# The last 32 rows of a graph layer's output projection, as one stacked float32r product

## The chip, the cores and the metric

The kernel runs on one core of one Trainium2 chip. The metric is the device time of one execution in microseconds (us), the median of the runs. Five engines work in parallel, each through its own queue in order: TensorE (PE, with its weight loads shown apart as PEld), VectorE (DVE), ScalarE (ACT), GpSimd (POOL) and SyncE (SP, which here only starts DMAs).

## The reference

The inputs are 625 nodes of 1024 features and 20,000 edges of two kinds. The part around the change is a relational graph layer and its output projection; a mixture-of-experts layer follows.

```python
def rgcn_conv(x, edge_index, edge_type, W_rel, W_root, bias):
    h_src = x[src]
    out = x @ W_root + bias
    for r in range(NUM_REL):                      # 2
        w = (edge_type == r).astype(x.dtype)
        msg = h_src @ W_rel[r] * w[:, None]
        sums = segment_sum(msg, dst, num_segments=N)
        cnt = segment_sum(w, dst, num_segments=N)
        out = out + sums / maximum(cnt, 1.0)[:, None]
    return out

y = elu(rgcn_conv(norm_x, ...))                   # 625 x 286  (D_FF = 286)
y = y @ wo_weight                                 # 286 x 1024
return hidden_states + y
...
x = x + _L0_gnn_ref(layernorm(x), ...)
x = x + _L0_ffn_ref(layernorm(x), ...)            # 8 experts, top 2, and 2 shared ones
```

All of it is float32. The contraction of the output projection has 286 rows: two full blocks of 128 and 30 more.

## The kernel before

The 625 nodes are five tiles of 125 rows (`TP = 125`, `NT = 5`). The work runs in these stages.

**Counting** (`one_hots`, `count_windows`, `count_out`, lines 823 to 892). The sums over edges are a product with a matrix of edge counts, CT. For 22 groups of edge columns (`GROUPS`) DVE makes two one-hot tiles, `oh_s` (lines 859 and 860) and `oh_k` (line 863), in a pool `oneh` of six buffers, and PE multiplies them (line 885, `cnt`). When a window of destinations is complete, `count_out` moves it: ACT to integers (line 826), DVE takes the digits apart with a bit mask (line 829), ACT copies them to CT (line 832). The loop calls `between(c)` after each of 160 edge columns c, and a table written by hand, filled with `at(c, f, ...)`, says what else is traced there: transposes of the normed rows, `project` (line 903, the products with the graph weights, fifteen of them, one every 18 columns in the middle of the stage), `add_h` (line 796), `aggregate`, and `clear`. The order on each engine is then fixed at build time from dependences and these places; `tc.issue_after(ins)` keeps an instruction behind another on its own engine.

`project` evicts a product in three steps: ACT to `rest` (line 912), ACT to the rounded `P` (line 913, float32r), DVE the remainder `rest - P` (line 914). So the graph sums already use float32r parts: the product `aggregate` (line 925) multiplies CT in float32r with both parts.

`clear` (lines 1011 to 1016, at column 50) sets the tile `zero` with POOL and writes zeros to the buffer `yt` in HBM with two DMAs of 2.5 MB on SP's queue.

**Aggregate and ELU** (lines 919 to 946). Each tile's sums are scaled and added on DVE; `elu` ends with ACT copying the last 30 columns a second time (line 945), so that the third block of `el` holds them twice, 32 columns apart.

**Output projection** (`elu_columns` and `output_proj`, lines 950 to 982). PE transposes `el` in three pieces (line 956), ACT copies them from PSUM to `eT` (lines 957 and 958), and `output_proj` multiplies per tile and half s of 512 columns: two blocks of 128 rows (line 968), then for both halves the last 30 rows (line 972), on two different groups of 32 rows of the array, the weights `wo_r` laid out to match. DVE adds each half to `xh` (line 975) and runs a layer norm (lines 732 to 736); POOL writes the rows out. The transposes of a normed tile (line 808, `p_t`) follow two tiles later. PE has as further work the shared experts' products (line 1159, `p_sh`), and the gate (line 1107) follows the last tile's transposes.

```python
for t, (c0, c1) in enumerate(((0, 3), (6, 11), (9, 14), (13, 18))):
...
at(50, clear)
...
for i, c in enumerate((3, 12, 15, 20, 38, 56, 74, 92, 110, 128, 146)):
    at(c, project, i + 1)
```

**After it** come routing, shared experts, eleven tiles of expert rows (`p_h`, line 1381; `p_yj`, line 1439) and the sum (`p_o`, line 1494, with a bf16 product of biases in line 1496). Their weights stream in on SP's queue, which starts again at 87.51 us, when the tiles of the `front` pool (node features, graph weights, one-hots, `zero`) are done with.

Of the kernel before, what the change touches and what calls it, by code (L numbers as in the profile page):

```python
# [8 lines left out]
F32 = mybir.dt.float32  # L9
F16 = mybir.dt.float16  # L10
BF16 = mybir.dt.bfloat16
F32R = mybir.dt.float32r
# [6 lines left out]
N = 625  # L19
D = 1024  # L20
E = 20000
R = 2
F = 286
# [3 lines left out]
TP = 125  # L27
NT = N // TP
# [14 lines left out]
QC = 32  # L43
# [16 lines left out]
def dense_kernel(  # L60
# [79 lines left out]
    wo_t = gbig.tile([FK, NFK, D], F32, name="wo_t")  # L140
    FL = F - 2 * FK
    nc.scalar.dma_start(wo_t[:, :2, :], wo[: 2 * FK].rearrange("(t p) m -> p t m", p=FK))
    nc.scalar.dma_start(wo_t[:FL, 2, :], wo[2 * FK :])

# [86 lines left out]

    CT = gbig.tile([128, NM, KEYS], F32, name="CT")
    PASSES = [(0, 418), (418, 418), (836, KEYS - 836)]

    def count_pass(i, between):
# [13 lines left out]
        for m in range(NM):  # L249
            if m % 2:  # L250
                nc.vector.tensor_copy(CT[:, m, c0 : c0 + cn], accs[m][:, :cn])
            else:
                nc.scalar.copy(CT[:, m, c0 : c0 + cn], accs[m][:, :cn])

# [22 lines left out]
    def aggregate(d, r):  # L277
        p = ps_mm(f"p_agg_{d}_{r}")
        at = r * N + d * TP
        for m in range(NM):  # L280
            n = rows_of[m]
            nc.tensor.matmul(p[:TP, : F + 1], CT[:n, m, at : at + TP], P[:n, m, r, :],
                             start=(m == 0), stop=(m == NM - 1))
# [21 lines left out]
    def output_proj(d):  # L305
# [6 lines left out]
        for s in range(2):  # L312
            cols = slice(s * 512, (s + 1) * 512)
            p = ps_acc(f"p_y_{d}_{s}")
            for k in range(NFK):
                n = FK if k < NFK - 1 else FL
                nc.tensor.matmul(p[:TP, :], eT[:n, k, :], wo_t[:n, k, cols],
# [136 lines left out]
def sparse_kernel(  # L454
# [24 lines left out]
    nc = tc.nc  # L479

    def pool(stack, name, bufs=1, side="left", **kw):
        return stack.enter_context(tc.tile_pool(name=name, bufs=bufs, side=side,
                                                reuse_waits="tile", **kw))
# [11 lines left out]
    def ps_acc(name):  # L495
        return psum[0].tile([128, 512], F32, tag="acc", name=name, bufs=nacc[0])

    def ps_mm(name):
        return psum[0].tile([128, 512], F32, tag="mm", name=name, bufs=3)
# [5 lines left out]
    gbig = pool(gnn, "gbig")  # L505
    gsum = pool(gnn, "gsum")
    rows = pool(gnn, "rows", NT)
    grow = pool(gnn, "grow", 2)
# [2 lines left out]
    crow = pool(cnts, "crow", 2)  # L511
    front = ExitStack()
    fbig = pool(front, "fbig", side="right")
    oneh = pool(front, "oneh", 6, side="right")


    PARTS = (slice(0, 112), slice(112, TP))
# [46 lines left out]
    ident = const.tile([128, 128], F32, name="ident")  # L564
# [61 lines left out]
    for i in (2, 3):  # L626
# [5 lines left out]
                                               ap=[[0, 3], [D, NS], [1, D]]))  # L632
    nc.gpsimd.dma_start(bd[:, NS:, :], bass.AP(tensor=b2.tensor, offset=b2.offset,
                                               ap=[[0, 3], [D, NE], [1, D]]))
# [18 lines left out]


    wo_t = gbig.tile([128, 2, D], F32, name="wo_t")
    FL = F - 256
    nc.sync.dma_start(wo_t, wo[:256].rearrange("(t p) m -> p t m", p=128))
    wo_r = gbig.tile([2 * QC, 512], F32, name="wo_r")
    for s in range(2):
        nc.sync.dma_start(wo_r[s * QC : s * QC + FL], wo[256:, s * 512 : (s + 1) * 512])  # L660


    nc.vector.tensor_scalar(low[:, 1], low[:, 0], 1.0 / DEG, 0.5 / DEG - 0.5, op0=ALU.mult, op1=ALU.add)
# [65 lines left out]
    def layernorm(row, h, name):  # L729
        st = small.tile([TP, 2, 6], F32, tag="st", name=name + "s")  # L730
        for s in range(2):
            nc.vector.bn_stats(st[:, s, :], row[:, s * 512 : (s + 1) * 512])
        mv = small.tile([TP, 2], F32, tag="mv", name=name + "m")
        nc.vector.bn_aggr(mv, st.rearrange("p a b -> p (a b)"))
        rstd = rsqrt(mv[:, 1:2], LN_EPS, name + "r")
        nc.vector.tensor_scalar(h, row, mv[:, 0:1], rstd, op0=ALU.subtract, op1=ALU.mult)
# [84 lines left out]


    CT = cbig.tile([TP, NT, R * N], F32R, name="CT")
    def count_out(d, n, acc):
        xi = crow.tile([TP, R * WD], I32, tag="xi", name=f"xi_{d}")[:, : R * n]
        nc.scalar.activation(xi, acc[:, : R * n], AF.Copy, scale=256.0)
        five = [TP, NT, R * n]
        ct = crow.tile([TP, NT, R * WD], I32, tag="ct", name=f"ct_{d}")[:, :, : R * n]
        nc.vector.tensor_tensor(ct, xi[:, None, :].to_broadcast(five),
                                mask[:, :, None].to_broadcast(five), op=ALU.bitwise_and)  # L830
        for r in range(R):
            nc.scalar.copy(CT[:, :, r * N + d : r * N + d + n], ct.rearrange("p t (d r) -> p t d r", r=R)[:, :, :, r])

# [83 lines left out]
    def aggregate(d, r):  # L919
# [3 lines left out]
        for m in range(NT):  # L923
            for i in range(2):
                nc.tensor.matmul(p[:TP, : F + 2], CT[:, m, at : at + TP], P[:, m, r, i],  # L925
                                 start=(m == 0 and i == 0), stop=(m == NT - 1 and i == 1))
# [7 lines left out]
    els = {}  # L934

    def elu(d):
        z = agg[:, d, :]
        lo = grow.tile([TP, F], F32, tag="lo", name=f"lo_{d}")
        nc.vector.tensor_scalar(lo, z, 0.0, None, op0=ALU.min)
        nc.scalar.activation(lo, lo, AF.Exp)  # L940
        el = grow.tile([TP, 256 + 2 * QC], F32, tag="el", name=f"el_{d}", bufs=3)
        nc.vector.memset(el[:, 256:], 0.0)
        nc.vector.tensor_scalar(el[:, :F], z, 0.0, None, op0=ALU.max)
        nc.vector.scalar_tensor_tensor(el[:, :F], lo, -1.0, el[:, :F], op0=ALU.add, op1=ALU.add)
        nc.scalar.copy(el[:, 256 + QC : F + QC], el[:, 256:F])
        els[d] = el

    eTs = {}

    def elu_columns(d):  # L950
        p = ps_mm(f"p_elT_{d}")
        pv = p[:, : 3 * TP].rearrange("p (k n) -> p k n", k=3)
        eT = grow.tile([128, 3, TP], F32, tag="eT", name=f"eT_{d}", bufs=NT - 1)
        for k in range(3):
            n = min(128, 256 + 2 * QC - k * 128)
            nc.tensor.transpose(pv[:n, k, :], els[d][:, k * 128 : k * 128 + n], ident[:TP, :TP])
        nc.scalar.copy(eT[:, :2], pv[:, :2])
        nc.scalar.copy(eT[: 2 * QC, 2], pv[: 2 * QC, 2])
        eTs[d] = eT

    h2s = {}

    def output_proj(d):
        eT = eTs[d]
        ps = [ps_acc(f"p_y_{d}_{s}") for s in range(2)]
        for s in range(2):
            for k in range(2):
                nc.tensor.matmul(ps[s][:TP, :], eT[:, k, :], wo_t[:, k, s * 512 : (s + 1) * 512],  # L968
                                 start=(k == 0), stop=False)
        for s in range(2):  # L970
            r = slice(s * QC, s * QC + FL)
            nc.tensor.matmul(ps[s][:TP, :], eT[r, 2, :], wo_r[r], start=False, stop=True)  # L972
        for s in range(2):
            at = slice(s * 512, (s + 1) * 512)
            nc.vector.tensor_add(xh[:TP, d, at], xh[:TP, d, at], ps[s][:TP, :])  # L975
        h2 = rows.tile([TP, D], F32, tag="h", name=f"h2_{d}")
        layernorm(xh[:TP, d, :], h2, f"ln2_{d}")
        h2s[d] = h2
        for g in PARTS:
            at = slice(d * TP + g.start, d * TP + g.stop)  # L980
            nc.gpsimd.dma_start(h2d[at, :], h2[g, :])
            nc.gpsimd.dma_start(x1d[at, :], xh[g, d, :])  # L982
# [18 lines left out]
    def at(c, f, *args):  # L1001
        after[c].append((f, args))
# [3 lines left out]
            at(c0, stats, t + 1)  # L1006
        at(c1, to_columns, t + 1, None, nT, True)

    zero = fbig.tile([128, D // 2], F32, name="zero")

    def clear():
        nc.gpsimd.memset(zero, 0.0)
        for a in range(2):
            to = bass.AP(tensor=yt.tensor, offset=yt.offset + (a * YB + 1) * D,
                         ap=[[NT * D, 128], [D // 2, 2 * NT], [1, D // 2]])
            nc.sync.dma_start(to, zero[:, None, :].to_broadcast([128, 2 * NT, D // 2]))

    at(50, clear)
    at(30, transpose_vec)
    at(10, scales, 2, 4)  # L1020
    at(14, scales, 4, NT)
# [12 lines left out]
    for d in range(NT - 1):  # L1034
        at(EC - 1, aggregate, d, 1)
        at(EC - 1, elu, d)
        if d > 1:
            at(EC - 1, elu_columns, d - 2)
# [393 lines left out]
    for n, j in enumerate(ORDER):  # L1432
        y = gat.tile([128, D], F32, tag="y", name=f"ys_{j}")
        for s in range(2):
            at = slice(s * 512, (s + 1) * 512)
            p = ps_acc(f"p_yj_{j}_{s}")
            for k in range(HK):
                for a, b, e in parts(j):
                    made = nc.tensor.matmul(p[a:b], hjT[:, j, k, a:b],  # L1439
                                     w2m[j, a, k][:, at] if a else w2a[:, bass.ds(e, 1), k, at],  # L1440
                                     start=(k == 0), stop=(k == HK - 1))
# [12 lines left out]
    for d in range(NT):  # L1454
        for a in range(2):
            at = a * YB + 1 + d * TP
# [24 lines left out]
    for d in range(NT):  # L1481
# [4 lines left out]
        for at in ((0, 512), (512, D)) if d < NT - 1 else ((0, 512), (512, 768), (768, D)):  # L1486
            n = at[1] - at[0]
            at = slice(*at)
            p = (ps_mm if banks % 8 > 4 else ps_acc)(f"p_o_{d}_{at.start}")
            banks += 1  # L1490
            with tc.issue_after(made.ins):
                for i in range(NS):
                    for k in range(HK):
                        nc.tensor.matmul(p[:TP, :n], shT[:, i, k, own], sw2[:, i, k, at],  # L1494
                                         start=(i == 0 and k == 0), stop=False)
# [10 lines left out]
def gnn_ffn_kernel(tc, *args):  # L1506
    nc = tc.nc
    with tc.tile_pool(name="flags", bufs=1) as flags:
        flag = flags.tile([1, 1], I32, name="flag")
        sparse_kernel(tc, flag, *args)  # L1510
        off = nc.values_load(flag, min_val=0, max_val=EC * 4 + 1)
        with tc.If(off > 0):
            dense_kernel(tc, *args)
# [31 lines left out]
```

## Time and profile before

| | |
|---|---|
| median of 3 runs | 298.7 us (298.64 to 299.25) |
| the profiled execution | 299.61 us, span 297.3 us |
| granted TensorE clock, mean | 0.995 |
| busy PE / DVE / ACT / POOL | 287.4 / 165.7 / 102.1 / 43.7 us |
| counting, from the first count to the last | 15.3 to 73.1 us |
| output projection, first product to last | 97.8 to 123.4 us |
| line 968 (two blocks of 128 rows) | 40 instructions in 5 tiles |
| line 972 (the last 30 rows) | 20 instructions in 5 tiles |

The span runs from the first to the last instruction; 2.3 us of the execution lie outside it. A float32 product is two PE instructions in the trace. Instructions on PE overlap, so the length of a run of them is read from the chain of waits, not from their own durations. "Idle before" names what ended the wait of an engine.

### The profile page before, as it was taken

What the parts mean: (1) busy time and instruction counts of PE and PEld (TensorE: products, weight loads), DVE (VectorE), ACT (ScalarE), POOL (GpSimd) and SP (SyncE); (2) the same over time, 40 slices, a digit from 0 to 9 for tenths busy, and PEclk for the clock granted to TensorE, in tenths of its full rate; (3) what the DMA queues carried; (4) which work ended last, traced back from release to release, by engine and by line L of the source; (5) the groups of instructions that cost most, each with busy time, mean ns of one, the idle gap of its engine ahead of it and who ended that gap; (6) DMA issues with size and microseconds to landing.
All of it is one profiled execution on the core that took longest, in us unless ns stands there. A gap on an engine that the chain in (4) does not pass through costs nothing.

```text
span 297.3 us, 4545 instructions
## 1 busy us (share of the span) xinstructions
PE 287.4 (97%) x1583; PEld 190.4 (64%) x1583; DVE 165.7 (56%) x458; ACT 102.1 (34%) x236; POOL 43.7 (15%) x97
## 2 busy tenths in 40 slices
PE   7999999999999999999999999999999999999991
PEld 5877777778888434567777887788743334444451
DVE  6799999998328588838980222132133221157920
ACT  2355115318325422435132553746289111000000
POOL 9400000000000034322021221210012222200000
PEclk9999999999999999999999999999999999999997
DMA  7999910000009999979997344420086545399251
GB/s 216 359 322 389 409 53 0 2 1 2 0 13 337 347 363 395 394 255 338 331 409 315 103 130 126 120 93 2 2 291 249 212 199 225 143 361 376 116 158 50
DMA packets 28657, 61.01 MB, mean 205 GB/s; under 512 B 2176, under 2 KB 16007, under 8 KB 28624
## 3 DMA queue, kind: packets, MB, share of 16 engines
q1 hardware_dynamic: 23102, 43.77, 41.7%
q0 software_dynamic: 5232, 16.55, 15.4%
q10 hardware_dynamic: 296, 0.35, 0.5%
q8 instruction: 15, 0.25, 0.4%
q14 instruction: 12, 0.10, 0.1%
HBM read 42.62 MB, written 18.81 MB: 207 GB/s over the span
## 4 chain that ended last, share of the span: by engine, by line
PE 82%; DVE 14%; ACT 1%; issue 1%; ACTq 0%; DVEq 0%
PE p_h L1381 13%; PE p_yj L1439 13%; PE p_o L1494 12%; PE p_sh L1159 11%; PE p_pr L908 10%; PE p_y L968 6%; PE p_agg L925 4%; PE p_x L1362 3%; DVE ohs L860 2%; DVE ohs L859 2%; PE p_t L808 2%; PE p_y L972 2%; PE scrap L988 2%; DVE st L765 2%; DVE xh L796 2%; DVE ohk L863 1%
## 5 line engine op out<-in xcount | busy, mean ns | idle before, releaser
L908 PE MATMUL p_pr<-wg,nT 128*125 128x286 f32 x240 | 62.1, 409 | 0.2
L908 PEld LDWEIGHTS p_pr<-wg,nT 128*125 128x125 f32 x240 | 43.3, 187 | 12.1 <-ACT nT L814 1.1
L1381 PE MATMUL p_h<-w1a,xsT 128*128 (+2 forms) x176 | 40.0, 380 | 0.0
L1439 PE MATMUL p_yj<-w2a,hjT 128*128 (+2 forms) x88 | 38.6, 594 | 0.0
L1494 PE MATMUL p_o<-sw,shT 128*125 128x512 f32 (+1 forms) x88 | 36.1, 553 | 0.0
L1159 PE MATMUL p_sh<-h2T,sw 128*128 128x313 f32 (+1 forms) x128 | 35.2, 428 | 0.0
L1381 PEld LDWEIGHTS p_h<-w1a,xsT 128*128 128x128 f32 (+2 forms) x176 | 28.7, 168 | 7.4 <-issue 0.5
L1159 PEld LDWEIGHTS p_sh<-h2T,sw 128*128 128x128 f32 x128 | 23.7, 189 | 8.6 <-issue 0.2
L1439 PEld LDWEIGHTS p_yj<-w2a,hjT 128*128 128x128 f32 (+2 forms) x88 | 14.4, 168 | 22.4 <-issue 22.4
L1494 PEld LDWEIGHTS p_o<-sw,shT 128*125 128x125 f32 x88 | 16.4, 187 | 16.9 <-issue 16.2
L1443 DVE COPY ys<-p_yj 128x512 f32<-128x512 f32 x15 | 10.4, 692 | 28.7 <-PE p_yj L1439 27.1
L1385 DVE COPY hj<-p_h 128x256 f32<-128x256 f32 x11 | 4.7, 425 | 31.1 <-PE p_h L1381 31.1
L982 POOL DMA_DIRECT2D x1d<-xh x10 | 5.4, 540 | 95.7 <-DVE xh L975 95.7
L1447 POOL DMA_INDIRECT yt<-ys,row x11 | 10.8, 981 | 50.5 <-DVE ys L1443 50.5
L968 PE MATMUL p_y<-wo_t,eT 128*125 128x512 f32 x40 | 18.1, 595 | 0.0
L1354 POOL DMA_INDIRECT xs<-h2d,tok x11 | 10.6, 961 | 45.6 <-PE p_x L1362 30.9
L1396 ACT ACTIVATE hjT<-p_hT,vT 128x128 f32<-128x128 f32 (+2 forms) x34 | 8.7, 332 | 24.5 <-PE p_hT L1393 24.5
L1366 DVE COPY xsT<-p_x 128x512 f32<-128x512 f32 x11 | 7.6, 692 | 17.0 <-PE p_x L1362 14.7
L1470 DVE SCALAR_TENSOR_TENSOR x<-p_o,x 125x512 f32<-125x512 f32 (+1 forms) x11 | 6.9, 641 | 16.3 <-PE p_o L1496 16.3
L925 PE MATMUL p_agg<-P,CT 125*125 125x288 f32 x100 | 15.6, 306 | 0.0
L912 ACT ACTIVATE rest<-p_pr,sc 125x286 f32<-125x286 f32 x10 | 5.0, 500 | 29.5 <-PE p_pr L908 22.0
L1381 PE MATMUL p_h<-w1m,xsT 128*64 128x256 f32 (+1 forms) x96 | 14.7, 381 | 0.0
(306 smaller groups left out, 423.8 us busy)
## 6 DMA issues: line engine op xcount, KB each, us to landing
w1a<-in_L_ffn_W_dram SPq DMA_DIRECT2D x8, 1024.0 KB, 12.1
w2a<-in_L_ffn_W_dram SPq DMA_DIRECT2D x8, 1024.0 KB, 6.5
yt<-zero SPq DMA_DIRECT2D x2, 2560.0 KB
g<-yt SPq DMA_DIRECT2D x10, 512.0 KB, 7.2
sw<-in_L_ffn_sW_dram SPq DMA_DIRECT2D x4, 1024.0 KB, 5.0
x<-x1d SPq DMA_DIRECT2D x5, 500.0 KB
wg<-in_L_gnn_W_rel_dram SPq DMA_DIRECT2D x2, 1144.0 KB, 17.1
x1d<-xh POOLq DMA_DIRECT2D x5, 448.0 KB, 6.4
```

The costliest lines, as they stand in the source:

```text
L908: nc.tensor.matmul(p[:TP, :F], nT[:, k, m * TP : (m + 1) * TP], wg[:, k, r, :], start=(k == 0), stop=(k == KD - 1))
L925: nc.tensor.matmul(p[:TP, : F + 2], CT[:, m, at : at + TP], P[:, m, r, i], start=(m == 0 and i == 0), stop=(m == NT - 1 and i == 1))
L968: nc.tensor.matmul(ps[s][:TP, :], eT[:, k, :], wo_t[:, k, s * 512 : (s + 1) * 512], start=(k == 0), stop=False)
L1159: nc.tensor.matmul(p[:, : z - a], sw1[:, i, k, t * 128 : (t + 1) * 128], h2T[:, k, a:z], start=(k == 0), stop=(k == KD - 1))
L1354: nc.gpsimd.indirect_dma_start(out=xs, out_offset=None, in_=h2d, in_offset=bass.IndirectOffsetOnAxis(ap=tok[:, j : j + 1], axis=0))
L1362: nc.tensor.transpose(p[:, k * 128 : (k + 1) * 128], xs[:, at : at + 128], ident)
L1381: nc.tensor.matmul(p[a:b, :H], xsT[j][:, k, a:b], w1m[j, a][:, 0, k, :] if a else w1a[:, bass.ds(e, 1), k, :], start=(k == 0), stop=(k == ...
L1396: nc.scalar.activation(hjT[:, j, t, a:b], p[:, t * 128 + a : t * 128 + b], AF.Gelu, bias=bT[:, bass.ds(e, 1), t])
L1439: made = nc.tensor.matmul(p[a:b], hjT[:, j, k, a:b], w2m[j, a, k][:, at] if a else w2a[:, bass.ds(e, 1), k, at], start=(k == 0), stop=(k = ...
L1443: nc.vector.tensor_copy(y[:, at], p)
L1447: sent.append(nc.gpsimd.indirect_dma_start(out=yt, out_offset=bass.IndirectOffsetOnAxis(ap=row[:, j : j + 1], axis=0), in_=y, in_offset=No ...
L1494: nc.tensor.matmul(p[:TP, :n], shT[:, i, k, own], sw2[:, i, k, at], start=(i == 0 and k == 0), stop=False)
```

## The change

The last rows become 32 instead of 30: the second block of 128 rows is cut to 126 (rows 128 to 253), and rows 254 to 285 form the third. `el` holds these 32 columns four times, so one transpose puts them on all 128 partitions. The copy `eR` is float32r, and on its upper 64 partitions DVE replaces the rounded value by the remainder. The weights `wo_r` are loaded four times over, rounded by ACT, and POOL replaces the second and the fourth group of 32 rows by the remainder. One float32r product of 128 rows then sums all four combinations of parts. Each half s gets its three products in a row, where before the last rows of both halves came at the end.

The weights' parts are made in `last_rows`, at column 78: for each half a DMA fills `zero` (now also the buffer of the load), ACT rounds it, behind the last copy to CT traced until then, and POOL subtracts twice on 32 partitions. `clear` moves from column 50 to 82. The pool of one-hots goes from six buffers to five. `clear` itself, all stages after the output projection and all other shapes are as before.

```diff
-    oneh = pool(front, "oneh", 6, side="right")
+    oneh = pool(front, "oneh", 5, side="right")
...
-    FL = F - 256
+    FL = F - QC
     nc.sync.dma_start(wo_t, wo[:256].rearrange("(t p) m -> p t m", p=128))
-    wo_r = gbig.tile([2 * QC, 512], F32, name="wo_r")
-    for s in range(2):
-        nc.sync.dma_start(wo_r[s * QC : s * QC + FL], wo[256:, s * 512 : (s + 1) * 512])
+    wo_r = gbig.tile([128, D], F32R, name="wo_r")
+    zero = fbig.tile([128, 512], F32, name="zero")
+
+    def last_rows():
+        for s in range(2):
+            at = slice(s * 512, (s + 1) * 512)
+            nc.sync.dma_start(zero, bass.AP(tensor=wo.tensor, offset=wo.offset + FL * D + s * 512,
+                                            ap=[[0, 4], [D, QC], [1, 512]]))
+            with tc.issue_after(outs[-1].ins):
+                nc.scalar.copy(wo_r[:, at], zero)
+            for g in (1, 3):
+                r = slice(g * QC, (g + 1) * QC)
+                nc.gpsimd.tensor_sub(wo_r[r, at], zero[r], wo_r[r, at])
...
         for r in range(R):
-            nc.scalar.copy(CT[:, :, r * N + d : r * N + d + n], ct.rearrange("p t (d r) -> p t d r", r=R)[:, :, :, r])
+            outs.append(nc.scalar.copy(CT[:, :, r * N + d : r * N + d + n],
+                                       ct.rearrange("p t (d r) -> p t d r", r=R)[:, :, :, r]))
...
-        el = grow.tile([TP, 256 + 2 * QC], F32, tag="el", name=f"el_{d}", bufs=3)
-        nc.vector.memset(el[:, 256:], 0.0)
+        el = grow.tile([TP, FL + 128], F32, tag="el", name=f"el_{d}", bufs=3)
...
-        nc.scalar.copy(el[:, 256 + QC : F + QC], el[:, 256:F])
+        nc.scalar.copy(el[:, F:].rearrange("p (g f) -> p g f", g=3),
+                       el[:, FL:F][:, None, :].to_broadcast([TP, 3, QC]))
...
-        eT = grow.tile([128, 3, TP], F32, tag="eT", name=f"eT_{d}", bufs=NT - 1)
-        for k in range(3):
-            n = min(128, 256 + 2 * QC - k * 128)
-            nc.tensor.transpose(pv[:n, k, :], els[d][:, k * 128 : k * 128 + n], ident[:TP, :TP])
-        nc.scalar.copy(eT[:, :2], pv[:, :2])
-        nc.scalar.copy(eT[: 2 * QC, 2], pv[: 2 * QC, 2])
-        eTs[d] = eT
+        eT = grow.tile([128, 2, TP], F32, tag="eT", name=f"eT_{d}", bufs=NT - 1)
+        eR = grow.tile([128, TP], F32R, tag="eR", name=f"eR_{d}", bufs=NT - 1)
+        for k, a in enumerate((0, 128, FL)):
+            nc.tensor.transpose(pv[:, k, :], els[d][:, a : a + 128], ident[:TP, :TP])
+        nc.scalar.copy(eT, pv[:, :2])
+        nc.scalar.copy(eR, pv[:, 2])
+        nc.vector.tensor_sub(eR[64:], pv[64:, 2], eR[64:])
+        eTs[d] = eT, eR
...
         for s in range(2):
+            at = slice(s * 512, (s + 1) * 512)
             for k in range(2):
-                nc.tensor.matmul(ps[s][:TP, :], eT[:, k, :], wo_t[:, k, s * 512 : (s + 1) * 512],
-                                 start=(k == 0), stop=False)
-        for s in range(2):
-            r = slice(s * QC, s * QC + FL)
-            nc.tensor.matmul(ps[s][:TP, :], eT[r, 2, :], wo_r[r], start=False, stop=True)
+                n = min(128, FL - k * 128)
+                nc.tensor.matmul(ps[s][:TP, :], eT[:n, k, :], wo_t[:n, k, at], start=(k == 0), stop=False)
+            nc.tensor.matmul(ps[s][:TP, :], eR, wo_r[:, at], start=False, stop=True)
...
-    zero = fbig.tile([128, D // 2], F32, name="zero")
...
-    at(50, clear)
+    at(78, last_rows)
+    at(82, clear)
```

## The prediction, made before the changed kernel was run

> **What bounds the kernel now.** I read the page first, then the chain of waits, then the timelines of the two stretches that the change touches. PE is busy for 287.4 of 297.3 us, so a change pays where it takes work from PE, or one of its few waits, and costs where it makes PE wait. The chain of waits through the last tile of the output projection, and three short runs from elsewhere in it:
>
> ```profile
> 77.07 1.33 PE p_agg L925 x10
> ...
> 118.94 3.44 PE p_y L968 x8
> 122.38 1.10 PE p_y L972 x4
> 123.48 0.68 DVE xh L975
> ...
> 127.64 0.82 DVE h L736
> 128.60 1.04 PE p_t L808 x8
> ...
> 258.22 0.22 PE p_o L1496
> ```
>
> A tile costs 3.44 us for its four full products, 0.86 each, and 1.05 to 1.10 us for the last 30 rows of both halves. The chain then leaves PE for DVE's layer norm; PE's own timeline shows what it does meanwhile:
>
> ```profile
> 123.36 1.96 PE L808 MATMUL p_t<-ident,h 125*128 125x125 f32 x16
> 125.16 2.80 PE L1159 MATMUL p_sh<-h2T,sw 128*128 128x313 f32 x10
> 128.60 1.04 PE L808 MATMUL p_t<-ident,h 125*128 125x125 f32 x8 [0.64 <-DVE h L736]
> ```
>
> Of DVE's 5.1 us only 0.64 is idle on PE. Now the middle of the counting stage, where the new weights' parts are made. The table by stretches (PE, PEld, DVE, ACT, POOL, then clock, DMA share and GB/s), PE's one wait there, and three lines of ACT's timeline:
>
> ```profile
> 37.00:58.00 21.00, 21.00 (x161) 16.27 (x159) 20.50 (x38) 7.51 (x20) 0.00 (x0) 1.00 0.06 23
> 58.36 0.36 PE L885 MATMUL cnt<-ohk,ohs 125*128 125x58 f16 x7 [0.20 <-DVE ohk L863]
> 51.47 1.65 ACT L832 CAST CT<-ct 125x315 fp32r<-125x315 int32 x4
> 53.01 0.43 ACT L913 CAST P<-rest 125x286 fp32r<-125x286 f32 x1
> ...
> 60.28 0.50 ACT L912 ACTIVATE rest<-p_pr,sc 125x286 f32<-125x286 f32 x1 [3.97 <-PE p_pr L908]
> ```
>
> DVE is busy for 20.5 of 21 us and its one-hots come just as PE takes them: the group of columns 104 to 111 is ready at 58.31 and PE had waited for it. ACT has room, DMA moves nearly nothing, POOL rests. Last, the only place where POOL reads two tensors while DVE works, from both engines' timelines (the third line is the same DVE form, alone):
>
> ```profile
> 7.38 0.67 DVE L778 TENSOR_SCALAR h<-xh,neg 125x640 f32<-125x640 f32 x1
> 7.42 0.26 POOL L625 TENSOR_TENSOR join<-ident 128x32 f32<-128x32 f32 x1
> 14.80 0.55 DVE L778 TENSOR_SCALAR h<-xh,neg 125x640 f32<-125x640 f32 x1
> ```
>
> **The change part by part.**
>
> *Last rows on PE.* A float32r product of 288 columns takes 0.133 us in a run (1.33 over 10), a bf16 one of 512 takes 0.22 (line 1496, between float32 products). By columns 0.133 gives 0.24; I take 0.225. A tile loses about 1.05 and gains 0.45: 0.60 saved, five times, 3.0 us. Cutting the second block to 126 rows I cost at nothing, since a run's length goes with columns. The weight loads (0.19) lie under the product before, as in line 1496's runs; should they not, it is at most 0.19 a tile. The third transpose loads 128 columns instead of 64: 140 against 110 ns, under 0.15 in all, partly hidden.
>
> *The wait at the end.* Half 0 is now complete 1.9 us (two products of 0.86 and one of 0.225) ahead of half 1, so its addition (0.68) and statistics (0.69) run beside half 1, and the norm ends 3.7 instead of 5.1 us after the last product. PE has 4.5 us to do there, so the 0.64 goes and no more. What is late next is DVE: its tile takes 4.65 us (107.52 to 112.2), PE's new one 3.9 plus 0.5 (transposes of `el`) or 1.0 (`p_t`). Laid out from 97.84, PE reaches the last `p_t` at about 124.9, and DVE's last norm, with two new subtractions of at most 0.35 (line 1110, 128x125 from PSUM), ends at 124.7. Before it was 128.60. Bounds: 0 to 0.64; I take 0.64.
>
> *Ahead of the first product.* ACT's copy of `el` grows from 30 to 96 elements, 0.217 to at most 0.256 us (line 958, 125 elements); `eR` is a copy like line 958's. DVE drops a memset of 0.11 and gains up to 0.35 per tile. Two of these may come in DVE's order before line 944 of the third tile, for which PE waits 0.61 at 96.93. Between 0 and 0.5 lost, I take 0.2. For tiles 3 and 4 `eR` is ready 6 us and more before its use.
>
> *Making the weights' parts.* On ACT: two copies of 128x512, 0.64 each (line 1375). The first comes behind the copies to CT that end at 53.12 and line 913, when ACT has nothing until 55.34: nothing lost. On SP: two loads of 256 KB replace two of 60; the second waits until POOL has read `zero`. Behind it on SP stand `clear`'s two DMAs, issued at 18.57 before and now after the last subtraction and POOL's memset (0.54), near 65. They took 5.7 us to issue and move 5.2 MB, 14 us at the 375 GB/s of the later loads; the queue has nothing else until 87.51, and `yt` is wanted after 217. Were that cover gone, the shared weights (line 1078), issued by 100.9 and landing 5.0 us later, would have 19 us until their first use at 125.16, more than the 14. The early DMAs lose `clear`'s traffic, which stood behind them: no gain counted. Fewer one-hot buffers: in the trace each group's line 859 begins after the group five before it was used; the closest is the one begun at 41.8, whose fifth predecessor is done at about 41.7. So nothing, at most 0.2.
>
> On POOL: four subtractions of 32x512, reading two tensors. The row is line 627, 128x32 in 0.266 us; the Trainium skill, "GPSIMD Engine Reference", section "Performance versus the Vector engine", gives 4497 ns for 2048 elements, which with that row is 2.1 ns an element, 1.27 us each (an estimate). POOL has the time. DVE may not. The row: with POOL's 0.26 beside it, line 778 took 0.67, alone 0.55, so DVE lost 0.12, 45% of POOL's time. The skill, "SBUF — State Buffer", section "Who interferes with whom", speaks against this change: a DVE instruction with two SBUF inputs and a GpSimd instruction that reads SBUF exclude each other for the whole instruction. Lines 859, 860, 863, 796 and 914 all have two. By the rule DVE loses 1.27 per subtraction, by the row 0.57, and 0 if POOL's reads fit in DVE's gaps. The first pair falls at about 54 to 57, where DVE has no slack: what it loses, PE waits. The second falls past 61; the next group (ready 64.05, used 64.60) has 0.55 of slack. So the cost is 2h + max(0, 2h - 0.55): 0 for h = 0, 1.7 for 0.57, 4.5 for 1.27. I take the row: it is one pair, but of this chip.
>
> **Sum.** -3.0 - 0.64 + 0.2 + 1.7 = -1.7 us. Against the profiled execution's 299.61 this is 297.9; that one stood 0.9 above the median, and I subtract from the median: 297.0.
>
> **The rivals.**
>
> *No collision.* POOL's reads cost DVE nothing. For it: DVE's two-input rows were never seen beside POOL's. Then -3.4: 295.3.
>
> *The port held for the whole subtraction*, the slower case. At 54 to 57 and 61 to 64 DVE's one-hots wait 1.27 us for each subtraction, PE behind them: -3.44 + 4.5 = +1.1, 299.8. It decides from h = 1.0, where 4h - 0.55 equals the gain. For it stands the rule; against it the row, whose DVE instruction lost less than half of POOL's time.
>
> *ACT's queue held.* ACT's second copy waits for the second load, behind it the eviction that starts at 60.28, then DVE's line 914 and the one-hots. If DVE keeps POOL out until it stops itself at 61.3, two subtractions (2.5), a load (3.9 us for 512 KB of `xh`), the copy and lines 912 and 913 follow: about 7.5 us of PE waiting, 302.8 or more. The lead of the second copy, which I put near 60, is about nothing, so half a us of this may come in any case.
>
> *The stacked product isn't cheap.* Were float32r two passes of 0.43, a tile would save 0.19 instead of 0.60, and the sum be +0.35: 299.1. Line 925's 0.133 us for 288 columns speaks against it.
>
> **How the numbers follow.** What a measurement here can tell from no change is about 0.2%, 0.6 us: faster is below 298.1, slower above 299.3. Partial collision, h from 0.3 to 0.8, gives 296.0 to 298.0: 0.40, the likeliest. No collision, 294.7 to 296.0: 0.25. Port held, 298.1 to 300.4: 0.20, of which 0.07 lies within 0.2%. ACT held, over 300.4: 0.09. Product not cheap: 0.06, mostly same. That makes faster 0.66, same 0.12, slower 0.22. The range 294.8 to 300.4 leaves out ACT's case and the edges.
>
> **What would show it.** Right: a run of two float32r instructions per tile near 0.22 each in place of line 972, tiles of 4.4 to 4.9 us, PE's wait for line 736 near zero, the last `p_t` 3.4 us nearer to the first `p_y`. For the collision: lines 859 to 863 longer than 0.68 and 0.39 beside POOL's four subtractions, and PE waiting for `ohk` between 55 and 65. Wrong: PE waiting for `ohk` by 4 us or more, or ACT idle before the second copy while line 912 is due; or the four subtractions beside DVE rows of unchanged length, and a time near 295.

## The result, and the profile after

The change made the kernel slower: 302.63 us median (301.52 to 303.84), beside 298.75 us for the kernel before on the same chip, a ratio of 1.0125 [1.0081, 1.0169]. In a second set of runs (e9 below) it was 302.45 against 299.03, ratio 1.012 [1.0071, 1.017]. 297.0 was predicted. The profiled execution took 301.66 us (span 299.9) at a mean clock of 0.988, where before had 0.995.

First the chain of waits of the changed kernel, from the last long run of the aggregate to the first tile of the output projection (start, length, what):

```profile
89.12 6.53 PE p_agg L938 x49
...
96.88 0.30 DVE eR L972
...
97.95 0.30 DVE eR L972
...
99.78 0.45 ACT lo L953
...
100.75 0.27 ACT el L957
101.02 0.07 ACT deg L940
...
101.13 0.20 PE p_deg L719 x2
101.33 3.47 PE p_y L984 x4
104.80 0.36 PE p_y L985
105.16 1.72 PE p_y L984 x4
106.88 0.23 PE p_y L985
```

Before, the same place read:

```profile
97.64 0.20 PE p_deg L709 x2
97.84 3.63 PE p_y L968 x8
101.47 1.05 PE p_y L972 x4
```

Two things stand out in the chain of the changed kernel. The new product (line 985) is cheap: 0.23 us for a half tile at 106.88, where before took 1.05 for both halves of line 972. But the full products of the first half tile take 3.47 us, those of the second 1.72: for that stretch PE ran at half its speed. The mean granted clock from 101.30 to 104.80 us is 0.53; in the 4.3 us before it is 1.00. The row of granted clock on the page of the changed kernel has a dip in the same place (before, all slices but the last were 9):

```profile
PEclk9999999999999799999999999999999999999997
```

Next PE's timeline, the rows in which it waited by 0.8 us or more after the start of the counting stage (idle time and releaser in brackets):

```profile
55.43 0.39 PE L898 MATMUL cnt<-ohk,ohs 125*128 125x58 f16 x8 [2.11 <-DVE ohk L876]
...
66.31 0.20 PE L898 MATMUL cnt<-ohk,ohs 125*128 125x24 f16 x2 [0.84 <-DVE ohk L876]
...
98.94 0.55 PE L969 MATMUL p_elT<-ident,el 125*128 125x125 f32 x3 [0.89 <-DVE el L956]
...
101.13 0.20 PE L719 MATMUL p_deg<-deg,onec 125*1 125x10 f32 x2 [1.64 <-ACT deg L940]
...
129.87 1.04 PE L818 MATMUL p_t<-ident,h 125*128 125x125 f32 x8 [0.93 <-DVE h L746]
```

Before, the longest from there on were 0.64 for `h` and 0.61 for `el`, and `p_deg` waited 0.20:

```profile
96.93 0.51 PE L956 MATMUL p_elT<-ident,el 125*128 125x125 f32 x3 [0.61 <-DVE el L944]
97.64 0.20 PE L709 MATMUL p_deg<-deg,onec 125*1 125x10 f32 x2 [0.20 <-ACT deg L927]
```

The first two waits of the changed kernel are for one-hots that came late. DVE's and POOL's timelines show why: POOL's subtractions (line 670) begin at 52.11 and at 60.53, and four groups of DVE instructions are longer than the same forms elsewhere, two of which are shown for comparison.

```profile
52.11 3.01 POOL L670 TENSOR_TENSOR wo_r<-zero,wo_r 32x512 fp32r<-32x512 f32 x2 [41.12 <-ACT wo_r L667]
60.53 3.54 POOL L670 TENSOR_TENSOR wo_r<-zero,wo_r 32x512 fp32r<-32x512 f32 x2 [5.41 <-ACT wo_r L667]
```

```profile
52.25 1.75 DVE L873 TENSOR_TENSOR ohs<-ohs,cols 125x1024 f16<-125x1024 f16 x1
53.92 1.46 DVE L876 TENSOR_TENSOR ohk<-iota,cols 125x464 f16<-125x464 f16 x1
...
57.47 0.68 DVE L873 TENSOR_TENSOR ohs<-ohs,cols 125x1024 f16<-125x1024 f16 x1
58.07 0.39 DVE L876 TENSOR_TENSOR ohk<-iota,cols 125x464 f16<-125x464 f16 x1
...
61.43 1.51 DVE L927 TENSOR_TENSOR P<-rest,P 125x286 fp32r<-125x286 f32 x1
62.86 2.36 DVE L872 TENSOR_TENSOR ohs<-iota,cols 125x1024 f16<-125x1024 f16 x2
```

1.75 against 0.68, 1.46 against 0.39, and by other rows of the same timeline 1.51 against 0.44 and 2.36 against 1.28: each subtraction cost DVE 1.07 or 1.08 us, whatever the instruction beside it. That is 2.09 ns for each of its 512 elements. While one of the two engines reads, the other waits; this is the shared port of which the prediction speaks.

So the change has two new costs ahead of the stage that it speeds up, and the stage's gain is there. The table puts the stages of the profiles side by side. The counting stage runs from the `p_t` for which PE waits near 28 us to the run of 49 `p_agg`; the start from there to the first `p_y`; the output stage from the first `p_y` to the last `p_t`. Lengths of stages can be compared even where the runs reached them at different times.

| | before | after | difference |
|---|---|---|---|
| counting | 27.99 to 87.44: 59.45 | 25.91 to 89.12: 63.21 | +3.76 |
| start of the output projection | to 97.84: 10.40 | to 101.33: 12.21 | +1.81 |
| output stage | to 128.60: 30.76 | to 129.87: 28.54 | -2.22 |
| `p_sh` done while PE waits for the last norm | 10 instructions | 8 | +0.53 later |
| sum | | | +3.88 |

The medians differ by 3.88 as well. That they agree so closely is luck. The two profiled executions themselves differ by only 2.05 us (301.66 and 299.61), because in the changed one these stages began 2.08 earlier: what lies ahead of these stages ended anywhere from 25.9 to 30.2 us in the profiles of this study, and 5.2 to 7.8 us lay between the start of the last addition and the end of the span, for all kernels. The experiments are therefore read by stage first, and by their medians second.

### The profile page after: what moved, and what is told of

Its sections match the earlier page's. It is cut to its first block, busy times and chain, and to the rows that moved or that the text cites. A ratio compares the mean times of both kernels' runs of the same rounds, so it can differ in the third digit from the quotient of the medians.

```text
span 299.9 us, 4534 instructions
## 1 busy us (share of the span) xinstructions
PE 283.9 (95%) x1573; PEld 190.4 (63%) x1573; DVE 171.3 (57%) x458; ACT 103.4 (34%) x238; POOL 50.2 (17%) x101
## 4 chain that ended last, share of the span: by engine, by line
PE 77%; DVE 18%; ACT 1%; issue 1%; ACTq 0%; DVEq 0%
PE p_h L1393 13%; PE p_yj L1451 13%; PE p_pr L921 13%; PE p_o L1506 11%; PE p_sh L1171 11%; PE p_agg L938 4%; PE p_x L1374 3%; PE p_y L984 2%; DVE ohs L872 2%; DVE ohs L873 2%; DVE xh L988 2%; DVE st L775 2%; PE scrap L1001 1%; DVE ohk L876 1%; DVE h L746 1%; PE p_t L818 1%
## 5 line engine op out<-in xcount | busy, mean ns | idle before, releaser
L984 PE MATMUL p_y<-wo_t,eT 128*125 128x512 f32 (+1 forms) x40 | 20.5, 637 | 0.0
L873 DVE TENSOR_TENSOR ohs<-ohs,cols 125x1024 f16<-125x1024 f16 (+1 forms) x22 | 14.9, 676 | 0.0
L872 DVE TENSOR_TENSOR ohs<-iota,cols 125x1024 f16<-125x1024 f16 (+1 forms) x22 | 14.7, 684 | 0.0
L938 PEld LDWEIGHTS p_agg<-P,CT 125*125 125x125 f32 x100 | 13.9, 187 | 0.8 <-DVE P L927 0.5
```

The source lines that it names most:

```text
L872: nc.vector.tensor_tensor(os, row[:, None].to_broadcast(shape), key, op=ALU.is_equal)
L873: last = nc.vector.tensor_tensor(os, os, both(VV_, 128)[1], op=ALU.mult)
L984: nc.tensor.matmul(ps[s][:TP, :], eT[:n, k, :], wo_t[:n, k, at], start=(k == 0), stop=False)
```

## The experiments

**e1 and e11: the change without POOL's subtractions.** The weights' low parts are left out, as in e3, in e10 and partly in e7, so these kernels show times and are no replacement for the change.

```diff
-            for g in (1, 3):
-                r = slice(g * QC, (g + 1) * QC)
-                nc.gpsimd.tensor_sub(wo_r[r, at], zero[r], wo_r[r, at])
```

> The changed kernel without POOL's four subtractions, so the low parts of the weights are not formed (groups 2 and 4 of wo_r hold the rounded value again). Theory: the subtractions keep DVE's two-input instructions waiting by 1.07 us each (lines 873, 876, 927 and 872 were longer by that beside them), and PE waited 2.11 + 0.28 + 0.84 = 3.2 us for one-hots; all of it goes: 302.6 - 3.2 = 299.4, with PE's wait for check's product (1.64 us) and the slow first product of the output projection still there. Rival, all of the loss lies in the wait ahead of the output projection: 302.6, the gaps in counting filled by something else. Rival, one-hots are late because of five buffers instead of six: gaps of 2 us in counting remain.

300.24 us (ratio to before 1.0031 [1.0009, 1.0053]). The counting stage is back at 59.53 us, and both waits for one-hots are gone. The wait for `deg` (1.65) and the slow half tile (3.48) remain. So POOL's subtractions are all of the counting stage's 3.7 us, and the other two belong to something else. The same kernel on another chip:

> The change without POOL's subtractions (the weights' low parts are left out) once more, on the chip of the other two. Theory: 300.2, 2.4 to 4 us below the change, with the first half tile at 3.47 us again. Rival (that half tile's 3.47 us was an accident of one run): 1.72 us, and 298.5.

300.37 us, 1.0041 [1.0007, 1.0075], with the slow half tile again.

**e2: the change, with `check` traced later.** The product `p_deg` sums the node degrees to see whether the edge list is as expected. In the changed kernel it stands ahead of the first `p_y`, and PE waits 1.64 us for it. The order on ACT has changed: before, its last copy of `deg` came right behind the fourth tile's exponential (`lo`, 97.10 to 97.54) and ahead of that tile's copy of `el`; now it comes behind both. ACT's timeline before:

```profile
97.10 0.44 ACT L940 ACTIVATE lo<-lo 125x286 f32<-125x286 f32 x1
97.45 0.14 ACT L927 COPY deg<-p_agg 125x1 f32<-125x1 f32 x1
98.07 0.22 ACT L945 COPY el<-el 125x30 f32<-125x30 f32 x1 [0.48 <-DVE el L944]
```

In the chain of the changed kernel `lo` ends at 100.23 and `deg` starts at 101.02.

```diff
-            check()
...
+        if s == 0:
+            check()
```

> The changed kernel with check(), whose one small product waits for the last copy to deg on ACT, traced after the first tile's output projection instead of before it. Theory: PE then waits only for the transposes of the third tile, 1.4 us less, and since it no longer stands nearly idle for 3 us the clock isn't lowered and the first half tile takes 1.72 instead of 3.47 us: together about 3.2, 299.4. Rival, the clock falls for another reason: 1.4 us only, 301.2. Rival, the port alone costs the time: 302.6.

303.46 us (1.0159 [1.0103, 1.0215]): no gain, where 299.4 was expected. Inside the trace the edit did its work: from the `p_agg` run to the last `p_t` it takes 38.43 us against 40.75. The clock fell in another place, in the counting stage, right after PE's wait of 2.11 us for one-hots at 56.07. Its row of granted clock:

```profile
PEclk9999999899999999999999999999999999999997
```

That fall cost little: the stage took 63.53 us beside 63.21 in the changed kernel. Its stages add up to +1.9 us over before, and the profiled execution was longer by 1.8 (301.40 beside 299.61); it was the fastest of four. The other three took 302.97 to 304.22 and left no trace, so why the median is 4.1 above before's is not explained, and the gain shows in the stages alone.

**e3: both edits.**

> Both edits: no subtractions on POOL (the weights' low parts are left out) and check() after the first tile's output projection. Theory: the two losses add, 302.6 - 3.2 - 3.2 = 296.2 or a little less, which is before's 298.75 minus the 3 us and more of PE work saved. Rival, one stall hides in the other: about 299.

297.04 us (0.9924 [0.9901, 0.9947]), with no dip in the clock row: counting 59.53, then 38.44 to the last `p_t` against 41.16 before. With both new waits away, the faster product is worth about 2 us.

**e4: the kernel before, with five one-hot buffers.**

> The kernel before with five one-hot buffers instead of six, nothing else. Theory: no group waits for a buffer, 298.75 within 0.5. Rival, DVE's lead is cut: over 299.5, with gaps before line 885 in counting.

298.97 us, 0.9994 [0.997, 1.0019]; counting 59.54. The smaller pool costs nothing, as the prediction had it.

**e7: less reading on POOL, one profile.**

```diff
-                nc.gpsimd.tensor_sub(wo_r[r, at], zero[r], wo_r[r, at])
+                if s == 0:
+                    half = slice(0, 256)
+                    nc.gpsimd.tensor_sub(wo_r[r, half], zero[r, half], wo_r[r, half])
+                else:
+                    nc.gpsimd.memset(zero[r], 0.0)
```

> One look at the port in the change: the first pair of POOL's subtractions is half as wide (32x256), and the second pair is replaced by two POOL memsets of 32x512 that read nothing (so part of the weights' low parts is left out). Theory (POOL holds the port for the elements that it streams, about 2.09 ns each): the DVE instruction beside each half-wide subtraction is 0.53 us longer, so ohs at line 873 takes about 1.2 and ohk at 876 about 0.9, and those beside the memsets are 0.68, 0.39 and 1.28 as without POOL. Rival A (a fixed hold per POOL instruction): 1.07 longer for the half-wide ones too. Rival B (POOL's writes hold DVE as well): 0.5 to 1.1 us longer beside each memset.

POOL's and DVE's timelines:

```profile
54.50 3.98 POOL L672 TENSOR_TENSOR wo_r<-zero,wo_r 32x256 fp32r<-32x256 f32 x2 [42.70 <-ACT wo_r L667]
64.26 1.09 POOL L674 MEMSET zero<- 32x512 f32 x2 [5.78 <-ACT wo_r L667]
```

```profile
56.14 1.75 DVE L810 SCALAR_TENSOR_TENSOR xh<-h,rstd,xh 125x1024 f32<-125x1024 f32 x1
57.82 0.98 DVE L931 TENSOR_TENSOR P<-rest,P 125x286 fp32r<-125x286 f32 x1
...
65.05 0.46 DVE L931 TENSOR_TENSOR P<-rest,P 125x286 fp32r<-125x286 f32 x1 [2.31 <-ACT P L930]
```

The half-wide subtractions held other instructions than expected (lines 810 and 931), but for the expected time: 0.47 (1.75 against 1.28 for line 810 at 52.47) and 0.52 (0.98 against 0.46). Half the elements, half the hold; so there is no fixed hold per instruction (1.8 to 2.1 ns an element). Beside the memsets line 931 takes its plain 0.46: POOL's writes held nothing here. What the hold is, is now settled; *when* POOL gets the port is not. Two half-wide subtractions took 3.98 us here, two whole ones 3.01 in the changed kernel: from POOL's start at 54.50 it was 1.6 us until the first DVE instruction that it held (line 810, 56.14), and DVE worked without a gap meanwhile.

**e6: ten products in the wait for `deg`.**

```diff
+        for _ in range(10):
+            nc.tensor.matmul(p[:, 128:256], ident, ident, start=True, stop=True)
```

> The change with ten extra 128x128 products on PE (their results are used by nothing) ahead of the check's product, in the 1.6 us in which PE waits for deg; nothing else differs. Theory (the first half tile of the output projection takes 3.47 instead of 1.72 us because PE had little to do in the 3 us ahead of it and its clock fell): it takes 1.72 us, the clock's row shows 9s there, and the time falls by up to 1.9 us, to about 300.8. Rival (the clock's fall follows from something else, such as the 2.1 us wait in the counting stage, or the products only lengthen PE's own work): no change or longer, 302.6 to 304.

305.61 us (1.021 [1.0147, 1.0273]), a miss in the total. The first half tile did speed up, to 1.91 us. But the counting stage, which the edit doesn't touch, took 64.66 instead of 63.21. POOL's, ACT's and PE's timelines of e6:

```profile
54.79 5.06 POOL L670 TENSOR_TENSOR wo_r<-zero,wo_r 32x512 fp32r<-32x512 f32 x2 [41.84 <-ACT wo_r L667]
```

```profile
64.78 0.62 ACT L667 CAST wo_r<-zero 128x512 fp32r<-128x512 f32 x1 [7.88 <-DMA zero<-in_L_gnn_wo_weight_dram]
...
65.83 0.43 ACT L928 CAST P<-rest 125x286 fp32r<-125x286 f32 x1
```

```profile
66.41 0.37 PE L940 MATMUL p_agg<-P,CT 125*125 125x288 f32 x1 [1.22 <-ACT P L928]
```

Here POOL got the port late. So it freed `zero` late, the second load came late, and ACT stood 7.88 us in front of its second copy, with the eviction of `project` queued behind; PE waited 1.22 us for that. This is the prediction's rival of ACT's queue, at a sixth of its price. e7 shows it too (1.33 us); the changed kernel's own profile does not.

**e10: the same ten products, without POOL's subtractions.**

> The change without POOL's subtractions (the weights' low parts are left out), and with the ten extra 128x128 products on PE in the wait for deg. Theory (the clock falls because PE has too little to do in those 3 us): first half tile 1.72 to 1.9 instead of 3.47 us; the products themselves end 0.5 later than the wait did, so 1.0 to 1.2 us less than the same kernel without them, about 299.2 beside 300.2. Rival (the clock's fall is a matter of the run): no difference between the two, or 0.5 more.

This is the clean test of the clock, beside e11 on the same chip: 298.08 us (0.996 [0.9929, 0.9991]) against 300.37 (1.0041 [1.0007, 1.0075]); the intervals don't meet. The chains of the two, e11 first:

```profile
99.61 3.48 PE p_y L981 x4
```

```profile
99.02 2.24 PE p_deg L717 x20
...
101.38 1.91 PE p_y L983 x4
```

Giving PE *more* to do made the kernel faster. From the `p_agg` run to the last `p_t` it is 39.57 instead of 40.63 us, the 1.1 expected; the medians differ by 2.3, and the other 1.2 isn't placed. The clock is on record for every run, not only for the two that left a trace: the mean of a run was 0.996 to 1.000 in all twelve of e10 and 0.984 to 0.993 in all twelve of e11. It was 0.994 to 1.000 in all twenty of e3, which has no wait for `deg`, and 0.983 to 0.993 in all twenty of e1, which has it.

**e9: the change once more.**

> The change once more, unaltered, for its spread on one chip beside the next two. Theory: POOL's four subtractions and DVE's instructions contend for the port, and when POOL gets it is a matter of how the two fall in time. Where POOL gets it at once, as in the change's first profile, the counting stage loses 3.8 us; where it gets it 1.6 us later, as in the profile with the products in the wait, the second load and with it ACT's second copy come late and the stage loses about 5.1 us. So the profile shows one of the two, 63.2 or 64.4 to 64.7 us from the first p_t after the wait for h to the p_agg run of 49, and the times spread over 2 us, 301.5 to 304. Rival (the longer stage belongs to the edit of those two runs, not to the change): 63.2 and 301.5 to 302.7.

302.45 us (301.06 to 303.92). The counting stage took 63.24 us, so the longer form didn't appear in this profile either; and the first half tile took 1.91 us:

```profile
103.35 1.91 PE p_y L984 x4
```

The waits ahead of it were the same, 0.88 and 1.65 us. So the clock's fall is not certain: of the five profiles with both of these waits and no extra products (after, e1, e7, e9, e11) four have it there. (The mean clock of this run was 0.993. The other five runs of e9 and the four of the changed kernel had 0.982 to 0.989, so those probably had it too.) Its price can be read from e9 against the first profile: 39.06 against 40.75 us to the last `p_t`, 1.7 us. Whether the 64.7 us of e6 also occur in the unaltered change stays open: both profiles are of short executions. Of its ten runs five took 301.06 to 301.84 us, these two among them, and five took 303.06 to 303.92, without a trace.

**e5: the whole change in another place.**

```diff
-    at(78, last_rows)
-    at(82, clear)
+    at(50, clear)
...
+    at(EC - 1, last_rows)
...
-            check()
...
+        if s == 0:
+            check()
```

> All of the change is kept, in another place: the weights' parts are made behind the last of the copies of counts (slot EC-1, where DVE has no one-hots left to make), clear goes back to slot 50, and the check of the degrees follows the first tile's output projection. Theory (port collision in the counting stage plus the check's product held on PE): the counting stretch is 59.5 us again as in before, POOL's four subtractions touch no one-hot, the first half tile runs at full clock, and the time is that of the run without subtractions and with the late check, about 297.0 (296.5 to 297.6). Rival (the parts cost their time wherever they stand, since something waits for them or for their loads): 299 or more, with PE waiting for wo_r at the first p_y or DVE's z and lo steps 1.07 us longer per subtraction and PE waiting for el.

298.05 us (0.9951 [0.9923, 0.998]), half a per cent below before and clearly below the change as it was, though 1.0 above what was expected. By stage it is e3 to the hundredth: counting 59.53, then 38.44. The 1.0 lies outside these stages and isn't explained. POOL's subtractions now run where DVE has no one-hots to make, and in 1.37 us each (POOL's timeline, the first pair; then DVE's, one line; then PE's, its longest wait):

```profile
78.02 2.73 POOL L670 TENSOR_TENSOR wo_r<-zero,wo_r 32x512 fp32r<-32x512 f32 x2 [66.05 <-ACT wo_r L667]
```

```profile
87.61 0.75 DVE L927 TENSOR_TENSOR P<-rest,P 125x286 fp32r<-125x286 f32 x1 [7.03 <-ACT P L926]
```

```profile
126.91 1.04 PE L818 MATMUL p_t<-ident,h 125*128 125x125 f32 x8 [1.74 <-DVE h L746]
```

The hold is still there: line 927 begins in the middle of a subtraction of the second pair and takes 0.75 instead of 0.46. But DVE has stood idle 7.03 us ahead of it, and PE doesn't wait. The 1.74 shows the next bound: DVE's layer norms.

**e8: e5, with the norm's last step on ACT** (for the last tile half on each engine).

```diff
-        nc.vector.tensor_scalar(h, row, mv[:, 0:1], rstd, op0=ALU.subtract, op1=ALU.mult)
+        if cut:
+            nc.vector.tensor_scalar(h[:, :cut], row[:, :cut], mv[:, 0:1], rstd, op0=ALU.subtract, op1=ALU.mult)
+        nb = small.tile([TP, 1], F32, tag="neg", name=name + "nb")
+        nc.vector.scalar_tensor_tensor(nb, mv[:, 0:1], -1.0, rstd, op0=ALU.mult, op1=ALU.mult)
+        nc.scalar.activation(h[:, cut:], row[:, cut:], AF.Identity, bias=nb, scale=rstd)
```

> The version of the run before the last two (parts made late, check after the first tile) with one more edit: the last step of the second layer norm, h = (x - mean) * rstd over 1024 columns, goes from DVE to ACT (for the last tile half on each). Theory (with the faster product DVE's norms bound the output stage, and PE's wait of 1.75 us for h at line 746 is their surplus): DVE loses 0.8 us per tile, the wait falls to under 0.6 and the time to about 295.7 (1 to 1.5 us below that version). Rival (ACT takes longer for it, 1.0 us or more, and the last tile's norm ends no earlier, or ACT's copies of h2T stand behind it): the same time or up to 1 us more, 297 to 298.

297.44 us (0.9942 [0.991, 0.9974]). In the profile the gate's first product comes 38.16 us after the `p_agg` run, in e5 39.49, so the step is worth 1.3 there: PE's wait for the norm falls from 1.74 to 0.74 us, though ACT takes 1.24 us per tile for what DVE did in 0.81. The medians differ by only 0.6, and the intervals overlap, so a gain over e5 isn't shown.

## Why the prediction was wrong

The sum said -1.7 us, and the stages give +3.9. Three of its steps failed. The hold h on DVE's one-hots was taken as 0.57 us and measured 1.07, which is 2.1 us of the miss. The start of the output stage was taken as 0.2 and measured 1.81, another 1.6, since the wait for `deg` was not seen. The fall of the clock behind that wait was put at nothing and cost 1.7. The small rest of the miss, 0.3, lies in the output stage. A right h alone would have moved the sum to +0.3, 299.0 us, which the prediction itself would have called the same.

**The product: right.** In e9, where the clock stayed up, the output stage took 26.86 us against 30.76, so 3.90 less. Of this 0.53 is `p_sh` work that only moved to a later place; 3.37 remain, and 3.64 were predicted (3.0 of products and 0.64 of the wait). A product took 0.23 where 0.225 was taken. That the transposes beside it also got shorter (`p_elT` 0.32 instead of 0.47) was not in the sum.

**The collision: the mechanism right, its size wrong.** This is the term h. The row chosen was one pair in which DVE lost 0.12 us beside a POOL instruction of 0.26, read as 45% of POOL's time, so 0.57 for one of 1.27. Measured: 1.07. The row could not carry this. Its DVE instruction (line 778) reads one tensor and a column of scalars, where the one-hots read two tensors, and its POOL instruction streams 32 elements, where the new one streams 512. Scaled by elements instead of by time, its 0.12 would have given 1.9, too much. It doesn't even repeat: in e4 line 778 begins at 7.53, beside the same POOL instruction (7.41 to 7.68), and takes its plain 0.55. The sum's own formula, 2h + max(0, 2h - 0.55), gives 3.73 with h = 1.07, and the stage lost 3.76. So the slack was right, and so were the places, and only h was not. The Trainium skill's page "SBUF — State Buffer", section "Who interferes with whom", against which the row was preferred, calls the port an exclusive lock, held for the whole instruction; the hold measured is 1.07 us of the 1.37 that an undisturbed subtraction takes in e5. It was nearer than the row: with its 1.27 the prediction's rival gave 299.8, still without the start and the clock.

**The start: 0.2 predicted, 1.81 measured.** This step looked at what DVE and ACT do for `el`, and found 0.28 of the loss (the wait for `el` grew from 0.61 to 0.89). It did not ask what PE has in line ahead of the first `p_y`. There stands `p_deg`, which had waited only 0.20 for its last `deg`. In the changed kernel the last `deg` comes behind `el` on ACT, which is 0.79 us of delay (100.23 to 101.02). And `lo` itself starts 4.13 us after the end of the aggregate's run where it was 3.14, with DVE's two new subtractions in that chain, 0.30 each (line 972). Together that is 1.78 of the 1.81; the wait for `deg` grew by 1.44. The bound of 0 to 0.5 was drawn around the edited instructions, not around the order that they stand in.

**The clock: not foreseen.** Before the first `p_y` PE was idle 0.89 and 1.64 us in a little over 3 us, and in four profiles of five the next half tile ran at half speed, 1.7 us lost. e10 shows that PE's idleness is the cause: filled with useless products, the wait is followed by products at full speed. So do e2 and e3, where the wait is gone and the first half tile is as short as the later ones. The skill's page "TensorE: Matmul & The Clock Gate", section "What's actually happening", gives a window of about 3.4 us of idling after which the clock halves. The traces agree with the halving (3.47 against 1.72) and with the time scale, but here it fell although PE was not fully idle, and in e9 with the same two waits it did not.

**The tail: half right.** The end of DVE's last norm was laid out at 26.9 us after the first `p_y`; e9 has 26.86 to the last `p_t`. But PE had got there earlier than laid out, with shorter tiles and two `p_sh` instructions fewer to do, and so waits 0.93, where the prediction let the whole 0.64 go. The two instructions come back later as 0.53.

**What cost nothing, as predicted:** five buffers (e4), the moved `clear` (in the changed kernel its two DMAs are issued at 64.68, and the weights behind them on SP at 89.16), and ACT's first copy.

With what was measured, the sum is -3.90 + 1.81 + 3.76 + 0.53 = +2.2, and +3.9 where the clock falls. The medians of the two sets of runs are +3.9 and +3.4; they hold what lies outside the stages too.

## What to carry to other kernels

A cost can be carried over from one pair of instructions to another only if the two pairs are alike in form and size; one pair with 32 elements and one input tensor said little of 512 elements and two. Where two estimates lie on either side of the point that decides the sign, the difference between them is what has to be measured first. Work moved into an idle engine belongs where its *neighbour* on the port has slack: the same four subtractions cost 3.7 us beside the one-hots, and by the stages nothing where the one-hots were done. When an edit lengthens the path to an engine's first instruction of a stage, look at every instruction already in that engine's queue and at the static order of those that feed it; and a wait of a few microseconds on PE may be followed by products at half speed, so it can cost more than its length.

## What the runs showed of the hardware

- A POOL subtraction that reads two tensors in SBUF (the on-chip memory) on 32 partitions held the two-input DVE instruction beside it by 1.07 us for 512 elements and by 0.47 and 0.52 for 256 (e7), whatever that instruction was. One that came in the middle of a subtraction lost less (0.29 in e5). POOL memsets of 32x512 held none (e7).
- POOL does not get the port at its first request: two subtractions took 3.01 us in the changed kernel and 5.06 in e6, with DVE's instructions in the same order. What decides is not seen in the trace.
- After two waits of 0.89 and 1.64 us within 3.1 us PE's next products took about twice their time in four of five profiles (3.47 instead of 1.72 us). Ten extra products in the second wait, 2.24 us of work, made a kernel 2.3 us faster by the medians and 1.1 by the stages (e10 beside e11).
- Without the two-group products of 32 rows, the transposes that follow were shorter: three `p_elT` 0.32 instead of 0.47 us. That the groups are the cause was not tested.
